# Hybrid block on one core: 128-row score stacks, single scatters per scan step, experts queued behind their last scatter

## The chip, the core and the metric

The kernel runs on one core of a Trainium2 chip. The metric is the device time of one launch in microseconds (us); for more than one run it is their median. TensorE (PE) multiplies matrices into PSUM and has a weight load of its own (PEld). VectorE (DVE), ScalarE (ACT) and GpSimd (POOL) do element-wise work. Each engine runs its instructions in the order of its own queue. Transfers are issued by SyncE (SP), and those with addresses taken from a tensor by GpSimd.

## The reference, cut to what matters

The input is x of 4 sequences x 512 tokens x 128 channels. Each `_layernorm` is over the channels.

```python
x = x + attn_a(layernorm(x), ...)      # state-space scan, then 8 experts, top 2 of each token
x = x + ffn(layernorm(x), ...)         # silu(gate) * up, then down; hidden size 384
x = x + attn_b(layernorm(x), ...)      # causal attention, 16 heads of 8
x = x + ffn(layernorm(x), ...)         # the same weights once more
```

In `attn_a` the scan keeps 256 channels x 16 states for each sequence, `h = dA*h + d*x*B` and `y = sum_n h*C`. Then a router picks two of eight experts for each token, and the output is the weighted sum of the two experts' outputs. In `attn_b` the scores of a head are q (8 numbers) times k (8 numbers), scaled, masked to the past, and put through a softmax.

## The kernel before, in words

**First stage, lines 599 to 1074.** One scan step belongs to one state of one sequence, so there are 4 x 16 = 64 of them, numbered 0 to 63 here. In `scan` (L895) VectorE runs the recurrence over all 2 x 512 positions (`hst`, L910), then the small operations of other work that was begun in this step, then the next step's input (`bx`, L889, which reads a PSUM tile `pb` and an SBUF tile). GpSimd multiplies `hst` by C (`hc`, L922), and TensorE sums the states (`yp`, L867). `hst` has two buffers, so scan step s+2 waits for `hc` of step s. `queued` (L875) makes every other GpSimd instruction traced between two `hc` run between these two. `hc` is also tied to run behind the last small VectorE operation begun in its step (L928).

**The work beside the scan.** Five `Stream` objects (L470) hold generators. In each scan step a stream whose last half-step is done begins its next generator piece, and later in the step ends it. Of the streams that want the PSUM tag "sc", only the first in order moves in a turn (`halves`, L575). The order is `ahead` (`front` of the next sequence: convolution, B and C, step sizes), `closing` (`close`: skip, gate, output projection, router, row numbers; then `start` and `scatter`), `tokens` (`combine`, `first_ffn`, `project`), `tiles` (`experts`, `onward`), and `rest`.

`scatter` (L254) sends each token's row to its two places in a DRAM tensor sorted by expert. That is 8 indirect DMAs for a sequence, issued by GpSimd, two per piece. `experts(g)` (L324) handles a group of sequences (group 0 is sequence 0, group 1 is sequence 1, group 2 is sequences 2 and 3), in 15, 15 and 23 tiles of 128 rows. It begins with `plan` (L270, where each tile begins) and `moved` (L302), then loads rows and the three weight matrices of each tile's expert through SP (L355 to L363), multiplies (L376, L388), and stores rows (L347). `start` (L584) puts it on the tiles stream ahead of `scatter`. `combine` (L395) gathers two rows for each token by 8 indirect DMAs, two per piece, and adds them to `base`. `project` (L502) writes q and k of a sequence, each split into three bf16 parts, to DRAM, and notes them in `stores`.

In `front`, `third` (L778) finishes the bf16 split of B and C in the tile `bc`: a copy of 32 rows (L779) and a subtraction (L780), both by GpSimd.

**Second stage, lines 1077 to 1330.** The heads of a sequence are treated in two units of 8 heads. `fill` (L1120) loads a unit's q and k parts into the stacks `qs` and `ks`, 96 rows high, of which 9 x 8 = 72 hold parts (`NP9`). `maxima` (L1131) multiplies 72 rows (L1145), adds the mask by another matmul (L1149), takes the row maximum with VectorE (L1141), and writes the maxima in three bf16 parts into rows 72 to 74 of `qs` (L1175). The same rows of `ks` hold -1 (L1103). `exps` (L1181) multiplies 75 rows (L1198, L1206) and takes the exponential (L1211). `weigh` (L1214) multiplies by the values (L1225). The streams go on: first whole turns until sequence 0 is in `stores` (L1287), then a turn beside 7 of 10 steps of `exps`, later 5 of 10, and forced turns where a sequence is not in `stores` yet (L1304). `last` is the final feed-forward of a sequence.

PE, VectorE, ScalarE and SP run in program order in the first stage (`ORDERED`, L34). GpSimd, and all engines in the second stage, are ordered by the scheduler.

Of the kernel before, what the change touches and what calls it, by code (L numbers as in the profile page):

```python
# [10 lines left out]
BF16 = mybir.dt.bfloat16  # L11
AF = mybir.ActivationFunctionType
ALU = mybir.AluOpType
# [3 lines left out]
P = 128  # L17
B, L, C = 4, 512, 128
NT = L // P
# [6 lines left out]
NH, HS, KVL = 16, 8, 64  # L26
# [11 lines left out]
def block_kernel(ctx, tc, x, rms1_w, rms2_w, in_proj_w, conv_w, conv_b, x_proj_w,  # L38
# [215 lines left out]
    def scatter(b):  # L254

        g = place[b][0]
        yield
        for t in range(NT):
            for k in range(2):
                done = nc.gpsimd.indirect_dma_start(  # L260
                    sorted_x[g], bass.IndirectOffsetOnAxis(ap=rows[b][:, t, k : k + 1], axis=0),
                    hs[b][:, t, :], None,
                ).ins
                tc.declare_no_dep(done, group=f"rows{g}", reason="no two tokens have the same row")
                tc.add_to_no_dep_group(f"rows{g}", done)
                if k and t < NT - 1:
                    yield
                    yield

# [54 lines left out]
    def experts(g):  # L324


        both, moved = plan(g)
        yield
        yield
        moved()  # L330
        yield
        yield
        n = NTILES[g]
        yield
        yield
        xt, xT, wgu, wd, hidden, ys, of = {}, {}, {}, {}, {}, {}, {}
        for i in range(-1, n + 3):
            if i == 0:
# [56 lines left out]
    def combine(b):  # L395

        g = place[b][0]
        got = []
        for t in range(NT + 2):
            for k, yk in enumerate(got.pop(0) if t > 1 else ()):  # L400
                nc.vector.scalar_tensor_tensor(
                    base[b][:, t - 2, :], yk, gates[b][:, t - 2, k : k + 1],
                    base[b][:, t - 2, :], ALU.mult, ALU.add,
                )
            yield
            new = []
            for k in range(2 if t < NT else 0):
# [5 lines left out]
                new.append(yk)  # L413
            got.append(new)
            yield


# [165 lines left out]

    def start(b):  # L584

        g, i = place[b]
        if i == len(GROUPS[g]) - 1:
            tiles.add(experts(g), onward(g))
        return
        yield  # L590

    def onward(g):
        for b in GROUPS[g]:
# [5 lines left out]
    with ExitStack() as first:  # L599
# [110 lines left out]
        def front(b):  # L710
# [65 lines left out]
                nc.scalar.copy(mid, rest)  # L776

            def third():  # L778
                nc.gpsimd.tensor_copy(bc[b][32:64, :], mid[32:64, :])  # L779
                nc.gpsimd.tensor_tensor(bc[b][64:96, :], rest[64:96, :], mid[64:96, :], ALU.subtract)  # L780

            if b == 0:
# [250 lines left out]
        with tc.manual_schedule(engines=ORDERED):  # L1033
            warm(16)
            moments(xs[0], mv0[:, 0])
            deviations([0])
            for k in range(KW):
                nc.vector.tensor_tensor(w_k[:, k, :], w_in[:, 0:EI], cwb[:, :, k], ALU.mult)
            first = front(0)
            next(first)  # L1040
            next(first)
            moments(xs[1], mv0[:, 1])
            deviations([1])


            w_bc = w1.tile([P, NE, 3, 2 * NS], F32, tag="w_bc", name="w_bc")
            nc.vector.tensor_copy(
                w_bc, w_xp[:, :, DTR:].unsqueeze(2).to_broadcast([P, NE, 3, 2 * NS])
            )
            pick32 = w1.tile([96, 2 * NS], F32, tag="pick32", name="pick32")  # L1050
            nc.vector.tensor_reduce(
                pick32, ident[0:96, 0:96].rearrange("p (g c) -> p c g", g=3), AX.X, ALU.add
            )
            pick = w1.tile([96, 2 * NS], BF16, tag="pick", name="pick")
            nc.vector.tensor_copy(pick, pick32)
            for _ in first:
                pass

            rest, ahead = Stream(early()), Stream()
            streams = [ahead, closing, tokens, tiles, rest]  # L1060
            for b in range(B):
                if b:
                    closing.add(close(b - 1), start(b - 1), scatter(b - 1))
                for n in range(NS):
                    if n == 0 and b + 1 < B:
                        ahead.add(front(b + 1))
                    if n == 8 and b == 0:
                        closing.add(prepared())
                    scan(b * NS + n, streams)
        with tc.manual_schedule(engines=ORDERED):  # L1070
            accumulate(*late.pop(0))
            closing.add(close(B - 1), start(B - 1), scatter(B - 1))
            for _ in range(3):
                turn(closing, tokens, tiles)


    with ExitStack() as second:
# [15 lines left out]

        NP9 = 9 * HS
        NU = NH // 2
        UNITS = 2 * B
        qs, ks = [], []
        for i in range(3):  # L1100
            qs.append(w1.tile([96, NU, L], BF16, tag=f"qs{i}", name=f"qs{i}"))
            k = w1.tile([96, NU, L], BF16, tag=f"ks{i}", name=f"ks{i}")
            nc.sync.dma_start(  # L1103
                k[NP9 : NP9 + 3, :, :], below.unsqueeze(1).to_broadcast([3, NU, L])
            )
            ks.append(k)

        def values(b):
            va, qk = vs[b % 2], stores[b][2]
# [10 lines left out]
        def fill(u):  # L1120

            b, h0 = u // 2, (u % 2) * NU
            q_d, k_d, _ = stores[b]
            for i in range(3):
                at = slice(3 * HS * i, 3 * HS * (i + 1))
                for stack, of in ((qs[u % 3], q_d), (ks[u % 3], k_d[i])):
                    nc.sync.dma_start(
                        stack[at], of[:, :, h0 : h0 + NU, :].rearrange("j d h l -> (j d) h l")
                    )

        def maxima(u):  # L1131
# [4 lines left out]
            for t in range(NT):  # L1136
                w = (t + 1) * P
                n = L // w
                for h0 in range(0, NU, n):
# [3 lines left out]
                    for h in range(h0, h0 + n):  # L1143
                        c = (h - h0) * w
                        nc.tensor.matmul(  # L1145
                            sc[:, c : c + w], q[0:NP9, h, t * P : w], k[0:NP9, h, 0:w],
                            start=(h == h0), stop=False, skip_group_check=True,
                        )
                    nc.tensor.matmul(  # L1149
# [22 lines left out]
            nc.scalar.copy(mT, pm)  # L1172
            m_d = dram.tile([3, NU, L], BF16, tag="m_d", name="m_d")
            nc.gpsimd.dma_start(m_d.rearrange("i h l -> (i h) l"), mT)  # L1174
            nc.gpsimd.dma_start(q[NP9 : NP9 + 3, :, :], m_d)  # L1175
            yield

        scale = float(HS) ** -0.5
# [2 lines left out]
        def exps(G):  # L1181
# [6 lines left out]
            for blocks in (  # L1188
# [198 lines left out]
```

## Time and profile before

| what | value |
|---|---|
| median of 3 runs | 919.38 us (919.25 to 921.01) |
| profiled execution, time | 916.44 us |
| profiled execution, span from first to last instruction | 914.7 us |
| mean granted TensorE clock | 0.872 |
| PE busy | 736.9 us (81%) |
| VectorE busy | 584.6 us (64%) |
| ScalarE busy | 409.4 us (45%) |
| GpSimd busy | 308.1 us (34%) |
| DMA, mean over the span | 108 GB/s |
| scan step 0, 24, 40, 48, 63 begins at | 38.1, 150.6, 232.8, 277.9, 377.1 us |
| first score matmul L1145 | 450.2 us |

Engine rows in the profile count busy time only, without the issuing of transfers. A line of the timeline begins with its start and its length in us; what stands in brackets at its end is how long the engine had been idle before it, and what ended that. In a table of windows, the columns behind the window are busy us of PE, PEld, VectorE, ScalarE and GpSimd with the number of instructions, then the granted TensorE clock (1.00 is full speed), the DMA share and GB/s.

### The profile page before, as it was taken

Reading aid. Unit: us, or ns where it says so; the run is one execution under the profiler, and the core shown is the slowest. Engines: PE = TensorE matmul, PEld = TensorE weight load, DVE = VectorE, ACT = ScalarE, POOL = GpSimd, SP = SyncE. Lnnn points to the kernel's source line nnn. Section 1 sums busy time; section 2 is a strip of 40 time slices with the busy share of each in tenths; the row PEclk is TensorE's granted clock in tenths of the full one; section 3 lists DMA queues with packets and bytes.
Section 4 is the critical chain, followed back from the end, with each engine's and each line's share of the span. In section 5 each row is a group of like instructions: output and inputs, shape, how many; then the busy total and the mean of one; then the engine's idle time right before and its main releaser. Section 6 shows DMA issues by size and latency. Waiting matters only on the chain. (4 is left out here: it accounts for less than half of the span.)

```text
span 914.7 us, 12164 instructions
## 1 busy us (share of the span) xinstructions
PE 736.9 (81%) x3867; PEld 436.0 (48%) x3867; DVE 584.6 (64%) x1160; ACT 409.4 (45%) x793; POOL 308.1 (34%) x242
## 2 busy tenths in 40 slices
PE   8698697699898855976696998898768997799854
PEld 4432242363466512564465576367524454365422
DVE  4799999899998987755364542275534266457311
ACT  3847556556743421342112553413436524546641
POOL 1165755765664467315103013000341402301010
PEclk9898999799999867998668999979968887989977
DMA  5167221361466314426735157627310420600000
GB/s 132 43 220 259 68 58 58 100 204 54 145 183 198 93 57 125 142 80 200 184 130 178 61 173 214 152 68 221 98 29 3 120 64 20 158 2 14 3 13 11
DMA packets 84481, 99.18 MB, mean 108 GB/s; under 512 B 10369, under 2 KB 56457, under 8 KB 83241
## 3 DMA queue, kind: packets, MB, share of 16 engines
q1 hardware_dynamic: 78881, 87.09, 32.4%
q0 software_dynamic: 4352, 10.89, 3.8%
q8 instruction: 31, 0.51, 0.2%
q10 hardware_dynamic: 1184, 0.43, 0.2%
q14 instruction: 33, 0.27, 0.1%
HBM read 76.67 MB, written 21.63 MB: 107 GB/s over the span
## 5 line engine op out<-in xcount | busy, mean ns | idle before, releaser
L922 POOL TENSOR_TENSOR hc<-hst,cs 128x1024 f32<-128x1024 f32 x64 | 150.7, 2355 | 132.1 <-issue 31.6
L867 PE MATMUL yp<-hc,ident 128*128 128x512 f32 x256 | 148.0, 708 | 48.6 <-POOL hc L922 47.4
L910 DVE TENSOR_TENSOR_SCAN hst<-da,bx 128x1024 f32<-128x1024 f32 x64 | 146.4, 2287 | 11.7 <-POOL hc L922 4.6
L1141 DVE TENSOR_REDUCE mx<-sc 128x1 f32<-128x384 f32 (+3 forms) x168 | 102.9, 636 | 59.5 <-PE sc L1149 57.4
L867 PEld LDWEIGHTS yp<-hc,ident 128*128 128x128 f32 x256 | 51.5, 216 | 129.4 <-POOL hc L922 89.3
L1211 ACT ACTIVATE p<-st 128x512 f32<-128x512 f32 x160 | 90.2, 598 | 30.0 <-PE st L1206 26.8
L847 ACT ACTIVATE da<-delta,A 128x512 f32<-128x512 f32 (+1 forms) x128 | 84.8, 714 | 34.3 <-DVE hst L910 26.6
L1145 PE MATMUL sc<-ks,qs 72*128 72x128 bf16 (+3 forms) x256 | 73.5, 347 | 14.8 <-DMA ks<-k_d 7.9
L321 DVE SCALAR_TENSOR_TENSOR thm<-thm,mpg 128x512 f32<-128x512 f32 x53 | 36.1, 681 | 68.1 <-ACT thm L382 68.0
L889 DVE TENSOR_TENSOR bx<-du,pb 128x1024 f32<-128x1024 f32 x64 | 78.2, 1223 | 2.0 <-PE pb L857 0.4
L376 PE MATMUL mpg<-xTm,wgu 128*128 128x128 f32 x424 | 66.9, 300 | 12.2 <-DMA wgu<-in_Wg_dram 7.7
L1198 PE MATMUL st<-qs,ks 75*128 75x512 bf16 (+3 forms) x256 | 63.6, 312 | 11.7 <-ACT p L1211 5.9
L376 PEld LDWEIGHTS mpg<-xTm,wgu 128*128 128x128 f32 x424 | 59.9, 212 | 21.9 <-issue 15.8
L1174 POOL DMA_DIRECT2D m_d<-mT x8 | 4.4, 552 | 183.6 <-ACT mT L1172 183.6
L376 PE MATMUL mpu<-xTm,wgu 128*128 128x128 f32 x424 | 62.7, 294 | 3.0 <-DVE mh L322 3.0
L369 ACT ACTIVATE xTm<-mpt,r2w 128x128 f32<-128x128 f32 x53 | 19.4, 366 | 100.7 <-PE mpt L367 100.7
L388 PE MATMUL mpd<-wd,mh 128*128 128x128 f32 x424 | 60.6, 287 | 1.9 <-ACT xTm L369 0.9
L376 PEld LDWEIGHTS mpu<-xTm,wgu 128*128 128x128 f32 x424 | 57.8, 210 | 5.6 <-DVE mh L322 3.3
L388 PEld LDWEIGHTS mpd<-wd,mh 128*128 128x128 f32 x424 | 54.2, 199 | 5.8 <-ACT xTm L369 3.3
L1149 PE MATMUL sc<-maskq,identb 128*128 128x128 bf16 (+2 forms) x176 | 49.3, 280 | 0.0
L382 ACT ACTIVATE thm<-mpg 128x512 f32<-128x512 f32 x53 | 31.7, 597 | 39.3 <-PE mpg L376 31.6
L321 DVE SCALAR_TENSOR_TENSOR th<-th,pg 128x512 f32<-128x512 f32 x24 | 16.5, 687 | 49.3 <-ACT th L449 49.2
(253 smaller groups left out, 1197.9 us busy)
## 6 DMA issues: line engine op xcount, KB each, us to landing
cs<-c_d SPq DMA_DIRECT2D x64, 256.0 KB
wgu<-in_Wg_dram SPq DMA_DIRECT2D x53, 256.0 KB
wgu<-in_Wu_dram SPq DMA_DIRECT2D x53, 256.0 KB
wd<-in_Wd_dram SPq DMA_DIRECT2D x53, 256.0 KB
xg<-zero SPq DMA_DIRECT2D x8, 1024.0 KB
qs<-q_d SPq DMA_DIRECT2D x24, 192.0 KB
k_d<-parts POOLq DMA_DIRECT2D x12, 384.0 KB
ks<-k_d SPq DMA_DIRECT2D x24, 192.0 KB
```

Source lines behind the costliest of these rows:

```text
L321: nc.vector.scalar_tensor_tensor(th, th, 1.0, g, ALU.add, ALU.mult)
L376: nc.tensor.matmul(pp[:, f, :], w[:, k, f * P : (f + 1) * P], rows_in, start=True, stop=True,)
L388: nc.tensor.matmul(pd, hT[:, f, :], w[:, f, :], start=(f == 0), stop=(f == NFC - 1))
L847: nc.scalar.activation(da[:, e, e:], delta[b][:, e, e:], AF.Exp, scale=A[:, e, n : n + 1])
L867: nc.tensor.matmul(yps[b][:, e, :], ident, hc[:, e, :], start=(n == 0), stop=(n == NS - 1))
L889: nc.vector.tensor_tensor(bxs[s], du[s // NS], taps[s][1].unsqueeze(1).to_broadcast([P, NE, L]), ALU.mult)
L910: nc.vector.tensor_tensor_scan(hst.rearrange("p e l -> p (e l)"), dec.pop(s).rearrange("p e l -> p (e l)"), bxs.pop(s).rearrange("p e l -> ...
L922: done = nc.gpsimd.tensor_tensor(hc, hst, cs.unsqueeze(1).to_broadcast([P, NE, L]), ALU.mult).ins
L1141: nc.vector.tensor_reduce(*taken, AX.X, ALU.max)
L1145: nc.tensor.matmul(sc[:, c : c + w], q[0:NP9, h, t * P : w], k[0:NP9, h, 0:w], start=(h == h0), stop=False, skip_group_check=True,)
L1198: nc.tensor.matmul(pt[:, c : c + L - kt * P], k[0 : NP9 + 3, h0 + j, rows], q[0 : NP9 + 3, h0 + j, kt * P : L], start=(c == 0), stop=False ...
L1211: ready[G] = nc.scalar.activation(p, pt, AF.Exp, scale=scale).ins
```

## The change

Four edits are made together.

1. `qs` and `ks` are 128 rows high. VectorE clears rows 64 to 127 of each of the six tiles when a stack is first filled. The maxima and the -1 rows are now rows 125 to 127. `maxima` multiplies 125 rows and `exps` all 128, with zeros in rows 72 to 124.
2. `scatter` moves on after every single scatter (for the last sequence after every two, as before), and `combine` of sequence 0 gathers one row per piece instead of two.
3. `experts` no longer plans. `plan` and `moved` go to the tiles stream ahead of the scatters, and `experts` and `onward` are put there behind the group's last scatter.
4. The copy of 32 rows of `bc` is done by ScalarE instead of GpSimd.

```diff
@@ scatter
-                if k and t < NT - 1:
+                if (k or b < B - 1) and (k, t) != (1, NT - 1):
                     yield
                     yield
@@ new, beside experts
+    def planned(g):
+        plans[g], moved = plan(g)
+        yield
+        yield
+        moved()
+        yield
@@ experts
-        both, moved = plan(g)
-        yield
-        yield
-        moved()
-        yield
-        yield
+        both = plans.pop(g)
         n = NTILES[g]
-        yield
-        yield
@@ combine
-        for t in range(NT + 2):
-            for k, yk in enumerate(got.pop(0) if t > 1 else ()):
+        n = 2 if b else 1
+        which = [(t, k) for t in range(NT) for k in range(2)]
+        for i in range(0, len(which) + 2 * n, n):
+            for yk, t, k in got[max(i - 2 * n, 0) : max(i - n, 0)]:
@@ start
-        if i == len(GROUPS[g]) - 1:
-            tiles.add(experts(g), onward(g))
-        return
-        yield
+        full = i == len(GROUPS[g]) - 1
+        if full:
+            tiles.add(planned(g))
+        yield from scatter(b)
+        if full:
+            tiles.add(experts(g), onward(g))
@@ third, in front
-                nc.gpsimd.tensor_copy(bc[b][32:64, :], mid[32:64, :])
+                nc.scalar.copy(bc[b][32:64, :], mid[32:64, :])
@@ scan loop, twice
-                    closing.add(close(b - 1), start(b - 1), scatter(b - 1))
+                    closing.add(close(b - 1), start(b - 1))
@@ stacks
-        NP9 = 9 * HS
+        NP9, MXR = 9 * HS, P - 3
-            qs.append(w1.tile([96, NU, L], BF16, tag=f"qs{i}", name=f"qs{i}"))
-            k = w1.tile([96, NU, L], BF16, tag=f"ks{i}", name=f"ks{i}")
-            nc.sync.dma_start(
-                k[NP9 : NP9 + 3, :, :], below.unsqueeze(1).to_broadcast([3, NU, L])
-            )
-            ks.append(k)
+            qs.append(w1.tile([P, NU, L], BF16, tag=f"qs{i}", name=f"qs{i}"))
+            ks.append(w1.tile([P, NU, L], BF16, tag=f"ks{i}", name=f"ks{i}"))
@@ fill
+            if u < 3:
+                for stack in (qs[u], ks[u]):
+                    nc.vector.memset(stack[KVL:P], 0.0)
+                nc.sync.dma_start(ks[u][MXR:P], below.unsqueeze(1).to_broadcast([3, NU, L]))
@@ maxima
-                            sc[:, c : c + w], q[0:NP9, h, t * P : w], k[0:NP9, h, 0:w],
+                            sc[:, c : c + w], q[0:MXR, h, t * P : w], k[0:MXR, h, 0:w],
-            nc.gpsimd.dma_start(q[NP9 : NP9 + 3, :, :], m_d)
+            nc.gpsimd.dma_start(q[MXR:P, :, :], m_d)
@@ exps
-                        pt[:, c : c + L - kt * P], k[0 : NP9 + 3, h0 + j, rows],
-                        q[0 : NP9 + 3, h0 + j, kt * P : L],
+                        pt[:, c : c + L - kt * P], k[:, h0 + j, rows],
+                        q[:, h0 + j, kt * P : L],
```

More of the change, by code (lines that the diff above doesn't have):

```diff
@@ L322, in halved @@
         nc.vector.scalar_tensor_tensor(dst, th, 0.5, other, ALU.mult, ALU.mult)
-    def experts(g):
-        both, moved = plan(g)
+    plans = {}
+    def planned(g):
+        plans[g], moved = plan(g)
         yield
@@ L331, in experts @@
         yield
-        yield
+    def experts(g):
+        both = plans.pop(g)
         n = NTILES[g]
-        yield
-        yield
         xt, xT, wgu, wd, hidden, ys, of = {}, {}, {}, {}, {}, {}, {}
@@ L397, in combine @@
         g = place[b][0]
+        n = 2 if b else 1
+        which = [(t, k) for t in range(NT) for k in range(2)]
         got = []
-        for t in range(NT + 2):
-            for k, yk in enumerate(got.pop(0) if t > 1 else ()):
+        for i in range(0, len(which) + 2 * n, n):
+            for yk, t, k in got[max(i - 2 * n, 0) : max(i - n, 0)]:
                 nc.vector.scalar_tensor_tensor(
-                    base[b][:, t - 2, :], yk, gates[b][:, t - 2, k : k + 1],
-                    base[b][:, t - 2, :], ALU.mult, ALU.add,
+                    base[b][:, t, :], yk, gates[b][:, t, k : k + 1], base[b][:, t, :],
+                    ALU.mult, ALU.add,
                 )
             yield
-            new = []
-            for k in range(2 if t < NT else 0):
+            for t, k in which[i : i + n]:
                 yk = wt.tile([P, C], F32, tag="yk", name="yk", bufs=6)
@@ L412, in combine @@
                 )
-                new.append(yk)
-            got.append(new)
+                got.append((yk, t, k))
             yield
@@ L1071, in block_kernel @@
             accumulate(*late.pop(0))
-            closing.add(close(B - 1), start(B - 1), scatter(B - 1))
+            closing.add(close(B - 1), start(B - 1))
             for _ in range(3):
```

## The prediction

> **What bounds the kernel now.** I read the table of windows first: from 40 to 320 us VectorE is busy 34 to 38 of every 40 us (32.4 and 26.4 in the two windows behind, where the scan ends), then TensorE takes over with 26 to 38 of 40. So the scan stage is read from the queues of VectorE and GpSimd, the second stage from TensorE and its clock.
>
> GpSimd's timeline where sequence 0 is scattered:
>
> ```profile
> 159.46 2.36 POOL L922 TENSOR_TENSOR hc<-hst,cs 128x1024 f32<-128x1024 f32 x1
> 161.99 1.01 POOL L260 DMA_INDIRECT xg<-hs,rows  x1 [0.17 <-issue]
> 163.30 0.96 POOL L260 DMA_INDIRECT xg<-hs,rows  x1 [0.30 <-issue]
> 165.90 0.97 POOL L779 COPY bc<-bc_mid 32x512 bf16<-32x512 bf16 x1 [1.64 <-DMA xg<-hs,rows]
> 166.93 1.15 POOL L780 TENSOR_TENSOR bc<-bc_rest,bc_mid 32x512 bf16<-32x512 f32 x1
> 168.16 2.35 POOL L922 TENSOR_TENSOR hc<-hst,cs 128x1024 f32<-128x1024 f32 x1
> ```
>
> VectorE's, of the same place:
>
> ```profile
> 163.00 2.29 DVE L910 TENSOR_TENSOR_SCAN hst<-da,bx 128x1024 f32<-128x1024 f32 x1
> ...
> 170.54 2.29 DVE L910 TENSOR_TENSOR_SCAN hst<-da,bx 128x1024 f32<-128x1024 f32 x1 [3.00 <-POOL hc L922]
> 172.75 3.68 DVE L833 TENSOR_TENSOR du<-du,sp_d 128x1024 f32<-128x1024 f32 x1
> ...
> 179.90 1.20 DVE L836 TENSOR_TENSOR delta<-delta,du 128x1024 f32<-128x1024 f32 x1
> ```
>
> A bare scan step lasts 3.75 us on VectorE (2.29 + 1.22 and gaps). Two scatters and a product are 4.82 us on GpSimd (154.64 to 159.46), and the bc pair waits until scatters have landed. The scan at 170.54 so waits 3.00 us, and `du` takes 3.68 where `delta`, of the same shape, takes 1.20: GpSimd's product ran from 172.99 to 175.34. For sequence 2, gathers join: products start at 335.93, 343.37, 350.81, 358.24, each 7.44 apart.
>
> The second stage, in the table of windows (busy PE, PEld, DVE, ACT, POOL; clock; DMA; GB/s):
>
> ```profile
> 446.00:450.00 4.00, 0.00 (x0) 0.00 (x0) 0.00 (x0) 0.00 (x0) 0.00 (x0) 0.50 0.80 189
> 450.00:454.00 4.00, 3.72 (x19) 2.20 (x20) 2.37 (x4) 0.00 (x0) 0.00 (x0) 0.50 0.86 178
> 458.00:462.00 4.00, 3.54 (x13) 1.52 (x12) 3.49 (x7) 0.00 (x0) 0.00 (x0) 0.50 0.91 292
> 462.00:466.00 4.00, 3.75 (x12) 1.40 (x11) 3.81 (x6) 0.00 (x0) 0.00 (x0) 0.50 0.00 0
> 466.00:470.00 4.00, 3.95 (x21) 3.34 (x20) 2.08 (x7) 0.37 (x1) 0.00 (x0) 0.50 0.02 4
> 474.00:478.00 4.00, 4.00 (x35) 3.65 (x35) 2.06 (x3) 1.37 (x5) 0.00 (x0) 1.00 0.63 193
> 875.00:880.00 5.00, 4.05 (x25) 1.19 (x26) 0.00 (x0) 1.41 (x3) 0.00 (x0) 0.52 0.00 0
> ```
>
> From 450 to 466 TensorE is 90% busy with 72-row score matmuls and stays at half clock. At 466.9 expert tiles with 128 rows begin, and within 5 us the clock is full.
>
> **The change part by part: single scatters.** One scatter and a product are 2.35 + 0.17 + 1.0 = 3.52 us, under 3.75, so GpSimd keeps up. For steps 24 to 33 I laid both queues out with the row durations. Before they run from 150.56 to 203.10. After, step 24 is as before; L780 waits for the scatter ahead of it (1.64 us after its issue here, 2.32 at 248.90), so `hc` of step 26 starts near 164.6, the queue behind it (next product, TensorE's sum, scan two steps on) is late, and one VectorE operation is still held, about 1.8 us; then nothing more. Step 34 begins at 194.9 instead of 203.1, or -8.2. Of it 4.6 is only work put off: four tiles' pairs L321/L322, 1.15 us each (4.90 - 3.75). Steps 40 to 47 took 45.1; their VectorE floor, with five tiles instead of six and the same 1.8, is 41.4: -3.7.
>
> Steps 48 to 62 took 99.2. After, summed from the same rows: step 48 6.0, 49 4.9, 50 9.0 (stall kept), 51 7.2, 52 4.9, 53 5.95 + 1.15, 54 4.4 + 1.15, 55 5.55 + 1.15, 56 and 57 4.9 each, 58 3.75, 59 with the plan 6.7, 60 4.5, 61 and 62 with scatter and gather 4.8 each: 85.8, or -13.4. The 7.44 us steps go; they did not need gathers so soon.
>
> **bc by ScalarE.** GpSimd loses 0.60 to 0.97 us three times in the scan; step 11 (`sp_d` held until 90.08) gains 0.7, the others lie inside the sums. ScalarE gains 0.5 to 0.6 each (nearest row: bc_mid, 0.61), hidden by its idle time (9.2 us before 179.23); without that cover 2 us. In the prologue one takes the other's place: 0, between -0.6 and +0.6.
>
> Scan step 63 so begins at 377.1 - 8.2 - 3.7 - 13.4 - 0.7 = 351, with 15 expert tiles done instead of 17 and `combine` of sequence 0 barely begun.
>
> **Experts later.** What was put off comes before attention. The built order has 14 tiles between scan and first maxima (before: 8), and 15 turns after the first three until sequence 0 is stored (before: 6). A turn with a tile costs 4.2 us by the nearest stretch: six tiles from 399.4 to 424.6, with close(3) and project(0) inside. SP's six transfers and two value loads of a tile (up to 5.3 us with a cs) move along with it, and three feed-forward turns without a tile cost 3.5 each. Sum: 15 x 4.2 + 10 + 3 (rest of the 7.2 us stall at 431.85, since scatters no longer sit between project's GpSimd steps) + 8 (stack loads, 442 to 450) + 5 (clears, below) = 89, against 73.1 before. The bounds are 3.8 a turn (tiles alone, 604 to 650: 12 in 46 us) and 6.6 (all turns from 377 to 437: 9 in 60). I take 4.2, since close(3) and project were inside it. First maxima: 351 + 89 = 440 instead of 450.2, with 29 tiles done instead of 25.
>
> To the fifth exponential group (656.3) it took 206.1 with 28 tiles; four fewer at 3.8 are -15.
>
> **128 rows.** The rows do not set a matmul's length: at full clock L1149 with 128 rows takes 0.38 for 512 columns, and so does L1198 with 75. In the maxima VectorE is busy 3.4 to 3.8 of 4 us, so there a faster TensorE gains little. The gain is behind them: tile work at half clock from 466.9 to 471.8 (2.2), L1225 at 585.1 (3.99 against 2.36: 1.6), tiles from 604 to 609.6 (2.2), 702 to 713 (11 us at half, I count 3), 760 to 766 (2.5, I count 1), L1225 at 876.9 (4.49 against 2.36: 2.1). That is 12, in three stretches of 6, 3 and 3. The Trainium skill (TensorE: Matmul & The Clock Gate, Part 1) says the full clock comes after about 3.4 us of sustained matmuls[...]. By that rule the gain is 0. The row above denies it: 16 us at 0.50 with 72 rows, full within 5 us with 128. But the added rows are zeros, and no row shows what zeros do to the clock. Bounds 0 to 16; I take 12, by the row. A loss is excluded as long as no wait is added.
>
> **Clears.** Six of 64 x 2048 elements: the nearest VectorE row is L889, 1.22 for 1024, so up to 2.4 each; GpSimd's clear of 1024 took 0.95. VectorE is busy 26.4 of 40 and 23.4 of 40 us there. Queued behind each are the tiles' L321 and L322, then L388; I put 5 on the path, bounds 0 to 15. The -1 rows' transfer on SP now waits for a clear, and weight loads are queued behind it: 0 to 6, inside the 5. Against it speaks a rule of the skill (SBUF — State Buffer, SBUF: two separate sides): a VectorE operation in a 2-port mode shuts GpSimd out for its whole length, also from writing descriptors. The row of `du` shows the lock the other way round. By the rule six clears delay GpSimd's scatters by up to 15, by GpSimd's rows (17.8 of 40 busy, 400 to 440) most falls in idle time. I add nothing.
>
> **Sum.** Span: 440 + 206.1 - 15.2 - 6 = 625 (before 656.3); to the ninth group 114.5 - 3 = 111.5; the rest 143.9 - 3 = 141. Together 877.5 against 914.7. The profiled execution adds 1.74 (916.44 - 914.7), and the median of the runs lies 2.94 above it: 882.
>
> **The rivals.** (A) The sum, 882, its own range 870 to 892, chance 0.50. (B) Zeros don't count for the clock, so the tall stacks do not do what they are there for: 894, chance 0.20; for it the rule, against it nothing but the row of real data. (C) The overlap is better: the five forced turns ahead of the seventh group are gone in the built order, and TensorE's idle 670.5 to 678.3 (yk gathers, then a norm) and the waits around it shrink: 15 less, 867, chance 0.17. (D) The turns before attention stay at 6.6 us, as they were with their chains through ScalarE and VectorE, and the clears come on top (15 / 18 = 0.8): 18 x 7.4 + 8 = 141 us instead of 89, so +52, 934; slower. It decides from 89 + 37 = 126 us, or 6.6 a turn with the clears' share in it ((126 - 8) / 18). Against it: the stretch at 4.2. Chance 0.08. (E) In between, 919: 0.05.
>
> **Numbers.** 882. Within 0.2% is about what this kernel's measurement can tell from no change. Range 862 to 904: A, B and C, leaving out D, E and the tails. Faster 0.88, same 0.03, slower 0.09.
>
> **What would show it.** `hc` of steps 25 to 32 about 3.8 us apart, `du` at 1.2; step 63 at 348 to 355; first L1145 at 430 to 450 with 29 tiles; granted clock above 0.5 in the maxima-only stretch and at the last L1225. Step 63 above 365 breaks the scan part; a first L1145 above 465 is D; clock 0.50 through the maxima is B.

## The result, and the profile after

The changed kernel takes 906.48 us, the median of 4 runs (901.97 to 908.82), beside 920.19 us for the kernel before on the same chip. The ratio is 0.9865, with a 95% interval of 0.9824 to 0.9906. It is faster by 1.35%, little more than a third of what was forecast (882 us, and 904 at the end of the range). The profiled execution took 908.82 us with a span of 907.1, the slowest of the four; in its trace the forecast span of 877.5 is missed by 29.6 us. Mean granted clock 0.895 (before 0.872), PE busy 715.0 us (before 736.9). The ratios here use executions in the chip's faster state alone, and the one profiled execution in its slower state, that of e3 below (919.67 us against a median of 910.85), is not used for the last stretch.

I read the trace of the changed kernel, called "after", stage by stage; `...` marks lines left out. First the scan, GpSimd's timeline where sequence 0 is scattered:

```profile
157.47 2.35 POOL L928 TENSOR_TENSOR hc<-hst,cs 128x1024 f32<-128x1024 f32 x1 [0.62 <-DVE bc_rest L781]
159.98 1.00 POOL L260 DMA_INDIRECT xg<-hs,rows  x1 [0.15 <-ACT bc_mid L782]
163.25 1.15 POOL L786 TENSOR_TENSOR bc<-bc_rest,bc_mid 32x512 bf16<-32x512 f32 x1 [2.27 <-DMA xg<-hs,rows]
164.48 3.40 POOL L928 TENSOR_TENSOR hc<-hst,cs 128x1024 f32<-128x1024 f32 x1
168.02 0.99 POOL L260 DMA_INDIRECT xg<-hs,rows  x1
169.03 2.37 POOL L928 TENSOR_TENSOR hc<-hst,cs 128x1024 f32<-128x1024 f32 x1
```

And VectorE's of the same place:

```profile
162.26 2.29 DVE L916 TENSOR_TENSOR_SCAN hst<-da,bx 128x1024 f32<-128x1024 f32 x1
...
167.91 2.29 DVE L916 TENSOR_TENSOR_SCAN hst<-da,bx 128x1024 f32<-128x1024 f32 x1 [1.10 <-POOL hc L928]
170.11 2.38 DVE L839 TENSOR_TENSOR du<-du,sp_d 128x1024 f32<-128x1024 f32 x1
```

The pair of scatters ahead of each product is gone, and the scan waits 1.10 us for `hc` where it waited 3.00. One wait of GpSimd is left, ahead of L786 (2.27 us), and `du` still takes 2.38 us beside a product. Scan step 63 begins at 356.51 (before 377.11).

Then the clears. This is VectorE in the norm of close(3), the last link before the router of sequence 3:

```profile
382.21 0.17 DVE L974 TENSOR_SCALAR rms_v<-ss 128x4 f32<-128x4 f32 x1 [1.51 <-ACT hs L967]
...
384.07 1.76 DVE L1128 MEMSET ks<- 64x2048 uint32 x1 [0.48 <-issue]
385.87 0.16 DVE L143 TENSOR_TENSOR rs_t<-rs_r 128x4 f32<-128x4 f32 x1
...
388.04 1.76 DVE L1128 MEMSET qs<- 64x2048 uint32 x1 [0.47 <-issue]
...
397.05 1.76 DVE L1128 MEMSET ks<- 64x2048 uint32 x1 [0.48 <-issue]
398.85 0.24 DVE L145 SCALAR_TENSOR_TENSOR rs_r<-rs_t,rs_r 128x4 f32<-128x4 f32 x2
```

TensorE's timeline behind it:

```profile
399.56 1.35 PE L176 MATMUL pt<-ident,hs 128*128 128x128 f32 x4 [10.83 <-ACT hs L977]
...
478.56 0.59 PE L1151 MATMUL sc<-ks,qs 125*128 125x128 bf16 x4 [5.52 <-DMA ks<-k_d]
```

The same chain in VectorE's timeline of before:

```profile
395.71 0.16 DVE L968 TENSOR_SCALAR rms_v<-ss 128x4 f32<-128x4 f32 x1
...
397.89 0.16 DVE L145 SCALAR_TENSOR_TENSOR rs_r<-rs_t,rs_r 128x4 f32<-128x4 f32 x1
```

Five of the six clears stand between `rms_v` and `rs_r`. Each costs 1.76 us and 0.48 us before it, and tile work slips in as well. The chain from `rms_v` takes 16.6 us from start to start, where it took 2.18 before. TensorE, in order, sits idle 10.83 us in front of the transpose that needs it. The first score matmul comes at 478.56, not at 440.

Last the clock, in the table of windows of after (columns as before: busy PE, PEld, VectorE, ScalarE, GpSimd; clock; DMA; GB/s):

```profile
482.00:486.00 4.00, 2.82 (x17) 1.48 (x16) 3.94 (x8) 0.00 (x0) 0.00 (x0) 1.00 0.95 216
486.00:490.00 4.00, 2.88 (x14) 1.35 (x14) 3.99 (x9) 0.00 (x0) 2.21 (x3) 1.00 0.84 262
...
615.00:620.00 5.00, 3.69 (x18) 1.73 (x18) 4.99 (x10) 0.00 (x0) 0.00 (x0) 1.00 0.00 0
```

In these stretches with maxima alone, where the clock was 0.50 before, it is now 1.00. TensorE is done early in them (2.8 of 4 us) and VectorE is the full engine (3.94 of 4).

### The profile page after: what moved, and what is told of

It reads as the page before. It is cut to its first block, busy times and chain, and to the rows that moved or that the text cites. A ratio compares the mean times of both kernels' runs of the same rounds, so it can differ in the third digit from the quotient of the medians.

```text
span 907.1 us, 12174 instructions
## 1 busy us (share of the span) xinstructions
PE 715.0 (79%) x3857; PEld 431.2 (48%) x3867; DVE 578.8 (64%) x1166; ACT 411.3 (45%) x797; POOL 307.7 (34%) x238
## 5 line engine op out<-in xcount | busy, mean ns | idle before, releaser
L873 PE MATMUL yp<-hc,ident 128*128 128x512 f32 x256 | 145.2, 695 | 47.7 <-POOL hc L928 45.5
L873 PEld LDWEIGHTS yp<-hc,ident 128*128 128x128 f32 x256 | 51.5, 215 | 128.4 <-POOL hc L928 87.2
L1217 ACT ACTIVATE p<-st 128x512 f32<-128x512 f32 x160 | 89.8, 599 | 38.6 <-PE st L1212 36.6
L1151 PE MATMUL sc<-ks,qs 125*128 125x128 bf16 (+3 forms) x256 | 66.1, 313 | 28.3 <-DVE mx L1147 19.3
L321 DVE SCALAR_TENSOR_TENSOR thm<-thm,mpg 128x512 f32<-128x512 f32 x53 | 36.2, 683 | 75.8 <-ACT thm L384 75.7
L378 PEld LDWEIGHTS mpg<-xTm,wgu 128*128 128x128 f32 x424 | 58.9, 208 | 18.7 <-issue 8.4
L1204 PE MATMUL st<-qs,ks 128*128 128x128 bf16 (+3 forms) x246 | 58.9, 306 | 9.3 <-ACT p L1217 5.1
L413 POOL DMA_INDIRECT yk<-yg,rows_y x32 | 31.0, 970 | 91.6 <-DMA yg<-ym 61.9
L260 POOL DMA_INDIRECT xg<-hs,rows x32 | 33.6, 1049 | 45.9 <-DVE cmove L305 39.9
L321 DVE SCALAR_TENSOR_TENSOR th<-th,pg 128x512 f32<-128x512 f32 x24 | 16.5, 687 | 49.0 <-ACT th L452 49.0
```

Of the source, the lines that this page charges most:

```text
L378: nc.tensor.matmul(pp[:, f, :], w[:, k, f * P : (f + 1) * P], rows_in, start=True, stop=True,)
L873: nc.tensor.matmul(yps[b][:, e, :], ident, hc[:, e, :], start=(n == 0), stop=(n == NS - 1))
L1151: nc.tensor.matmul(sc[:, c : c + w], q[0:MXR, h, t * P : w], k[0:MXR, h, 0:w], start=(h == h0), stop=False, skip_group_check=True,)
L1204: nc.tensor.matmul(pt[:, c : c + L - kt * P], k[:, h0 + j, rows], q[:, h0 + j, kt * P : L], start=(c == 0), stop=False, skip_group_check=True,
L1217: ready[G] = nc.scalar.activation(p, pt, AF.Exp, scale=scale).ins
```

## The experiments

Each ratio is to the kernel before on the same chip; a difference of 1% is about 9.2 us. From each trace I took four moments: the start of scan step 63, the first expert tile whose `mh` is made after it, the first score matmul, and the end. They split what follows the scan into three stretches:

| kernel | step 63 | to first tile | tile to first score | first score to end | ratio to before (95%) |
|---|---|---|---|---|---|
| before | 377.1 | (overlap) | 73.1 in all | 464.5 | 1 |
| after | 356.5 | 18.2 | 103.8 | 428.5 | 0.9865 (0.9824 to 0.9906) |
| e1 clears by GpSimd | 354.7 | 18.2 | 93.3 | 426.9 | 0.9747 (0.9683 to 0.9811) |
| e2 stacks alone | 377.4 | (overlap) | 89.4 in all | 450.6 | 0.9995 (0.9972 to 1.0018) |
| e3 no stacks | 355.2 | 18.2 | 87.2 | not used | 0.9905 (0.9881 to 0.9929) |
| e4 clears, 72 rows | 356.5 | 18.2 | 101.1 | 445.3 | 1.0035 (0.9996 to 1.0074) |
| e5 experts behind, alone | 375.5 | (overlap) | 87.3 in all | 470.1 | 1.0135 (1.0022 to 1.0248) |
| e6 gathers in pairs | 355.9 | 21.4 | 95.8 | 443.9 | 1.0028 (1.0005 to 1.0051) |
| e7 clears twice | 355.9 | 18.2 | 116.5 | 431.1 | 1.0060 (1.0033 to 1.0088) |
| e8 clears late | 354.7 | 18.3 | 105.5 | 423.2 | 0.9879 (0.9830 to 0.9927) |
| e9 last product first | 356.7 | 18.7 | 104.5 | 422.1 | 0.9851 (0.9810 to 0.9892) |
| e11 zeros by DMA, 53 rows | 357.4 | 18.5 | 125.8 | 473.2 | 1.0690 (1.0631 to 1.0750) |
| e12 GpSimd, in pieces | 356.4 | 18.2 | 91.6 | 429.3 | 0.9775 (0.9679 to 0.9871) |
| e13 the same, late | 355.7 | 18.2 | 94.9 | 430.9 | 0.9806 (0.9723 to 0.9890) |
| e14 DMA, 48 rows | 355.7 | 18.6 | 87.9 | 423.9 | 0.9628 (0.9572 to 0.9685) |
| e15 DMA, 32 rows | 354.0 | 18.6 | 87.7 | 426.2 | 0.9707 (0.9676 to 0.9738) |
| e16 DMA, 16 rows | 356.9 | 18.7 | 86.1 | 438.3 | 0.9786 (0.9754 to 0.9818) |
| e17 DMA, 48 and 5 rows | 354.0 | 18.6 | 94.6 | 430.4 | 0.9889 (0.9820 to 0.9958) |

**The edits taken apart.** Four kernels: clears moved to GpSimd; the stacks alone on the kernel before; the change without the stacks; the change with its clears but with 72 and 75 rows multiplied.

e1:

```diff
-                    nc.vector.memset(stack[KVL:P], 0.0)
+                    nc.gpsimd.memset(stack[KVL:P], 0.0)
```

> The changed kernel with its six clears issued on GpSimd instead of VectorE, nothing else. Theory T1 (the clears cost what they hold up: the norm behind close(3) took 16.6 us on VectorE with clears of 1.76 us between its links, 2.06 before, and TensorE idled 10.83 us behind it): that chain is short again, the idle 10.83 us before pt<-hs goes, the first score matmul comes 10 to 14 us before 478.6, the time falls to 892 to 897. Rival T2 (the order of turns sets the first score matmul, and the clears only fill time in which VectorE would have waited): first scores within 3 us of 478.6, time 903 to 910. Rival T3 (GpSimd is slow at clears and its scatters of sequence 3 wait behind them, above 20 us): 915 or more.

0.9747 (893.37 us), first scores at 466.2: T1. But GpSimd's clears are not free either. VectorE's timeline of e1:

```profile
380.72 3.45 DVE L136 TENSOR_SCALAR rs_t<-rms_v 128x4 int32<-128x4 int32 x1
...
384.20 3.46 DVE L139 TENSOR_SCALAR rs_r<-rs_t 128x4 int32<-128x4 int32 x2
...
388.04 0.68 DVE L321 SCALAR_TENSOR_TENSOR thm<-thm,mpg 128x512 f32<-128x512 f32 x1
```

GpSimd's:

```profile
380.60 3.54 POOL L1128 MEMSET ks<- 64x4096 bf16 x1
384.09 3.54 POOL L1128 MEMSET qs<- 64x4096 bf16 x1
```

Two integer links that take 0.17 us alone took 3.45, and each ends when a clear on GpSimd ends (384.1, 387.6). `thm`, at 0.68 us beside the next clear, was not held. This is the lock between VectorE and GpSimd of which the Trainium skill (SBUF — State Buffer, SBUF: two separate sides) says that whoever starts first keeps it for the whole instruction. The prediction asked what VectorE's clears do to GpSimd; here GpSimd's clears hold VectorE, the direction that its row of `du` had shown.

e2, the kernel before with edit 1 alone:

> The kernel before with the 128-row stacks and the clears by VectorE alone; scatters, gathers, bc and the start of the experts as before. T1: the clock gain of about 12 us and a cost of clears of 5 to 15 us before the first scores nearly cancel, 913 to 923, with the granted clock at 1.0 in the stretch with maxima alone (0.50 before, 450 to 466). T2 (clears free, clock gain whole): 905 to 909. If the rise of the clock is worth little because VectorE bounds the maxima: 921 to 932.

0.9995 (916.91 us): the two nearly cancel, as T1 had it. The first scores come 16.3 us later after step 63 than before (89.4 against 73.1), and the rest is 13.9 us shorter (450.6 against 464.5).

e3, the change without edit 1 (the stack lines of the diff undone):

> The changed kernel without the 128-row stacks and without the clears: 72 and 75 rows again, the other three edits kept. T1: loses the clock gain of 12 us and the cost of clears of about 12, so within 5 us of the changed kernel, 902 to 912, its first scores at 464 to 469 and the clock at 0.50 through its maxima. T2 (clears free): 916 to 921, first scores at 476 to 481.

0.9905 (910.85 us), within 0.4% of the changed kernel, as T1 had it: edit 1 as a whole brings next to nothing, since its gain is paid back by its clears. The first scores came at 460.7, some 3 us sooner than expected.

e4, the clears kept, the rows not used:

```diff
-        NP9, MXR = 9 * HS, P - 3
+        NP9, MXR = 9 * HS, 9 * HS
...
-                        pt[:, c : c + L - kt * P], k[:, h0 + j, rows],
+                        pt[:, c : c + L - kt * P], k[0 : NP9 + 3, h0 + j, rows],
...
```

The second operand is cut to 75 rows in the same way, and the -1 rows and the maxima go to rows 72 to 74.

> The changed kernel with tall, cleared stacks, but the -1 rows and the maxima back in rows 72 to 74 and the matmuls over 72 and 75 rows. Clears and order as in the changed kernel, so the difference to it is the granted clock alone. By the sum of the prediction 12 us slower than the changed kernel: 916 to 921, clock 0.50 in the maxima. Rival: TensorE's busy time fell by 21.9 us between the kernels, all of it counts: 926 to 930. Rival: VectorE or ScalarE bound these stretches: 904 to 909.

1.0035. The 922.91 us lie in none of the three ranges, nearest to the first (916 to 921). Against e3 the clears cost 1.3%, or 12 us; against the changed kernel the clock is worth 1.7%, or 15.6 us (16.8 in the traces behind the first score). The table of windows of e4, at the place of 615 to 620 above:

```profile
619.00:624.00 5.00, 4.47 (x17) 2.00 (x16) 4.27 (x9) 0.00 (x0) 0.00 (x0) 0.50 0.00 0
```

The same work, with 72 rows instead of 125: half clock.

**Experts behind the last scatter, alone** (e5, the kernel before with edit 3):

> The kernel before with one edit alone: the experts of a group begin behind its last scatter. Scatters and gathers stay in pairs, bc stays on GpSimd, the stacks stay at 96 rows. Theory T4 (the single scatters and gathers carry the gain in the scan): step 63 of the scan stays at 374 to 378, the first scores come about 104 us later (as without stacks and clears), near 480, and the whole takes 922 to 932. Rival (what the scan gains is only expert work put off, which this edit alone would put off too): step 63 near 357 to 366 and 908 to 914.

1.0135, slower. Step 63 stays at 375.5, as T4 had it, but this does not show what T4 concludes. At step 63 the trace of e5 has 17 tiles done, as many as before (15 in the changed kernel), so this edit alone put no tile off. By the prediction's 1.15 us for a tile's pair L321/L322, the two tiles put off in the changed kernel are 2.3 of the 20.6 us that its scan gained, an estimate; what the gathers and feed-forward pieces put off are worth was not measured. The opposite combination, single scatters without edit 3, was not run. My first scores at 480 were wrong: they came at 462.8.

**Gathers in pairs again** (e6, `n = 2` in `combine` for every sequence):

> The changed kernel with sequence 0's gathers in pairs again (all other edits kept). Combine of sequence 0 then takes four turns fewer, so attention begins about four turns earlier. If the first scores are late because of the turns before them (each 4.6 us with a tile in it, 84 us of the 104 without clears), they come at 458 to 464 instead of 478.6. Theory T1 on the total (the tiles put off are done later in the same time, TensorE is busy on both sides): time within 5 us of the changed kernel, 901 to 911. Rival (turns ahead of attention are lost time): 886 to 893. Rival (hc of step 63 is held longer by more gathers, nothing else): 908 to 913.

1.0028 (920.86 us), outside all three ranges, and the first scores came at 473.2, not at 458 to 464. The built order has four turns fewer before attention (11 instead of 15), and three turns forced in ahead of the seventh exponential group, for which sequence 2's projection isn't ready. The first scores come 5.4 us earlier, the rest takes 15.4 us longer. From the first score to the end, after and then e6 in the table of windows:

```profile
478.56:907.10 428.54, 344.50 (x2353) 214.75 (x2363) 211.86 (x561) 182.53 (x363) 72.84 (x81) 0.90 0.31 86
473.16:917.10 443.94, 359.10 (x2444) 226.81 (x2455) 217.24 (x568) 187.55 (x375) 72.85 (x81) 0.92 0.32 90
```

TensorE is busy 14.6 us longer in e6 and idle just as long (84.8 and 84.0 us). So it is the work put off that makes the rest longer (27 tiles are done before the first score, against 30), not waits around the forced turns. Single gathers are worth some 1.6%, though nearly nothing of that is saved in the scan (step 63 at 355.9). Why four turns fewer saved only 5.4 us before the first score stays open.

**Are the clears late enough, or dear anywhere?** e8 makes them wait for the last scatter; e7 does each twice.

```diff
...
-                    nc.vector.memset(stack[KVL:P], 0.0)
+                    ins = nc.vector.memset(stack[KVL:P], 0.0).ins
+                    tc.add_manual_dep(ins, last_scatter[0].name, behind, reason="clears late")
```

> The changed kernel with the six clears on VectorE made to wait for the last scatter of sequence 3, so that none can fall among the links of close(3)'s norm. T1: the norm is 2 to 4 us again, TensorE's idle 10.83 us is gone, first scores at 462 to 468, and since neither engine's clear blocks the norm, a bit better than clears on GpSimd, where integer links of the norm still took 3.45 us instead of 0.17: 886 to 893. Rival: the clears now hold up VectorE's tile work and the stack loads by as much: 899 or more.

0.9879 (905.79 us): no gain over the changed kernel, the rival's range. The norm was short again and the scatters began at 401.81 instead of 418.73, but the clears then fell into the feed-forward part. VectorE's timeline of e8:

```profile
416.41 1.76 DVE L1131 MEMSET ks<- 64x2048 uint32 x1 [0.48 <-DVE th L324]
418.21 0.69 DVE L325 SCALAR_TENSOR_TENSOR fh<-th,pu 128x512 f32<-128x512 f32 x1
```

TensorE's:

```profile
415.98 2.07 PE L451 MATMUL pg<-xT,fwg 128*128 128x512 f32 x2 [6.58 <-DVE th L324]
```

TensorE waits 6.58 us for `th`, which stands behind the first clear, and more behind the next ones. T1 in the form "only the norm's links cost" fell here: VectorE's queue is in order, and at both places something on TensorE's path stands behind the clears.

> The changed kernel with each of the six VectorE clears done twice. T1 (VectorE's clears lie on the path wherever they fall, since putting them behind the scatters changed nothing): 12 to 16 us more, 918 to 923, first scores at 490 to 496. Rival (only their place among the norm's links costs, and the second clear of each pair adds 1.8 us to it once or twice): 908 to 912.

1.0060, or 18 us above the changed kernel by the ratios (14.6 in the traces), with the first scores at 490.6: T1. A second set of six clears (13.4 us of VectorE's time with the gaps) costs 12.7 us in the stretch before the scores. In this stage a clear on VectorE costs nearly its whole length on the path.

**Clears on GpSimd in pieces** (e12: eight of 64x512 for each; e13: the same, behind the last scatter):

> Clears on GpSimd, each in eight pieces of 64x512. With whole clears two links of the norm (integer operations on VectorE, 0.17 us) took 3.45 us each, until a clear of GpSimd ended. Theory (a VectorE operation of that kind waits for the GpSimd instruction that runs, so it waits for a piece of about 0.5 us instead of 3.5): the chain of close(3) falls by 5 to 6 us, first scores at 460 to 462, 887 to 890. Rival (it waits for the whole row of clears, or the pieces cost more in all than they free): 893 to 900.

The mechanism held. VectorE's timeline of e12:

```profile
382.10 0.53 DVE L974 TENSOR_SCALAR rms_v<-ss 128x4 f32<-128x4 f32 x1 [1.28 <-ACT hs L967]
...
382.66 0.46 DVE L136 TENSOR_SCALAR rs_t<-rms_v 128x4 int32<-128x4 int32 x1
...
383.15 0.47 DVE L139 TENSOR_SCALAR rs_r<-rs_t 128x4 int32<-128x4 int32 x2
```

0.46 instead of 3.45, since a piece ends every 0.47 us. The operation held need not be an integer one: `rms_v`, a `TENSOR_SCALAR` in f32 (0.17 in the changed kernel), takes 0.53. The time did not follow: 0.9775, in the rival's range, and 91.6 us to the first scores against 93.3. Of the 6 us that the two links gained, 1.7 are left at the end of the stretch; where the others went was not traced.

> As the one before, with the pieces placed behind the last scatter of sequence 3 in GpSimd's queue, when GpSimd is idle but for one addition until project(0). Theory: no link of close(3) meets a clear, 885 to 889. Rival: 48 pieces of 0.5 us behind the scatters delay GpSimd's addition x<-base,fo and the projection of sequence 0, which is on the path: 895 or more.

0.9806 (899.50 us), in the rival's range; not told apart from e1.

**The last product** (e9: the scatter and gathers ahead of step 63's product put behind it):

> The changed kernel with the scatter and the three gathers that stand ahead of the last step's product put behind it. The product is at 360 instead of 364.56, and TensorE's last sum of the scan begins at about 363 instead of 366.95. If that chain (product, sum, y, out projection, norm) sets the first scores: they come 4 us earlier, 902.5 for the whole. Rival: the tiles' chain in the same turns sets it, no change: 906.5.

0.9851, no change (904.70 us). GpSimd's timeline of e9:

```profile
361.98 2.33 POOL L932 TENSOR_TENSOR hc<-hst,cs 128x1024 f32<-128x1024 f32 x1 [2.20 <-DVE base L406]
...
372.07 0.94 POOL L413 DMA_INDIRECT yk<-yg,rows_y  x1 [0.30 <-issue]
373.04 2.34 POOL L955 TENSOR_TENSOR y<-y,sz 128x1024 f32<-128x1024 f32 x1
```

The product is at 361.98 (364.56 in the changed kernel), but the gathers then stand ahead of `y`, which begins at 373.04 (372.26). GpSimd's queue has that work to do in any order.

**Zeros by DMA.** No engine clears; rows 72 onward are written from a small tile of zeros on SP's queue. e11 writes 53 rows a stack:

```diff
...
-                    nc.vector.memset(stack[KVL:P], 0.0)
+                    nc.sync.dma_start(
+                        stack[NP9:MXR], nought.unsqueeze(1).to_broadcast([MXR - NP9, NU, L])
+                    )
```

> The changed kernel with the rows 72 to 124 of the stacks zeroed by six DMAs from a small tile of zeros on SP's queue, no clear on VectorE or GpSimd. T1: no engine is held, the norm is 2 to 4 us, first scores at 461 to 467, 886 to 893. Rival: 2.6 MB more through the DMA engines (they are 13 to 85% busy there) and six more issues on SP ahead of the weights delay the tiles: 897 to 903.

1.0690 (978.68 us), far worse than either. SP's queue in e11:

```profile
412.04 14.94 SPq L1130 DMA_DIRECT2D ks<-nought  x1
427.03 18.07 SPq L1133 DMA_DIRECT2D ks<-below  x1
```

The table of windows there:

```profile
435.00:445.00 10.00, 0.00 (x0) 0.00 (x0) 0.00 (x0) 0.00 (x0) 0.00 (x0) 0.50 0.07 24
```

The DMA engines are 7% busy, about one of sixteen, and move 24 GB/s; 424 KB at that rate are 18 us, and the weights behind wait (TensorE idle for 27.15 us). The Trainium skill (DMA: Bandwidth & Descriptors, Why a DMA increments its semaphore by 16 and not by 1) says that a copy runs on the largest number of engines up to 16 that divides the size of the outermost dimension on both sides. For 53 rows that is 1, which agrees with the 7%. e14, e15 and e16 take 48, 32 and 16 rows:

> The changed kernel with zeros by DMA, 48 rows of them instead of 53 (120 rows in the maxima, 123 in the exponentials). If 53 rows went through one of the 16 DMA engines because 53 does not divide among them (7% busy, 24 GB/s), 48 rows go at 150 GB/s or more, 2.6 us each, TensorE's wait of 27 us is gone, no engine clears, and first scores come 87 to 91 us behind the first tile after the scan, as without clears: 885 to 892, the clock as with 125 rows. Rival (rows of 1 KB from a broadcast source are slow whatever their number): 960 or more.

0.9628: 886.84 us, as the first case had it, the best version found and faster than both kernels. The rival is out. SP passes the two transfers in 1.4 us:

```profile
411.16 0.75 SPq L1130 DMA_DIRECT2D qs<-nought  x1
411.97 0.65 SPq L1130 DMA_DIRECT2D ks<-nought  x1
```

The stretch to the first scores is 87.9 us, as without clears (87.2 in e3). So the zeroing costs next to nothing by itself; the in-order engine that did it cost 16 us. The clock did not do all that was expected of it, as the table below shows.

> As the one before with 32 rows of zeros: 104 rows in the maxima, 107 in the exponentials. If the clock needs only somewhat more than 75 rows: as with 48, within 4 us. If the clock asks for nearly all rows: the maxima stay at 0.50 and the time is 12 to 17 us above that of 48 rows.

0.9707. By the medians 3.0 us above e14 and in the trace 2.3 behind the first score, the first case; by the ratios 7 us, between the two cases. The clock of its first maxima was mostly 0.50.

> As the one before with 16 rows of zeros: 88 rows in the maxima, 91 in the exponentials. If the number of rows counts by degrees, the maxima lie between 0.50 and 1.00 here; if there is a step, they show one of the two. Time 900 to 906 with the clock at 0.50, 885 to 892 at 1.00.

0.9786 (897.09 us, some 3 under the range for a clock of 0.50): 14.4 us behind e14 after the first score. The first maxima show 0.50, as with 72 rows, yet 88 rows are worth something: the stretch behind the first score is 7.0 us shorter than with 72 rows in e4 (438.3 against 445.3), and the ratio is 1.2% below that of e3.

e17 has 125 and 128 rows again, with transfers of 48 and 5 rows:

> The changed kernel with its full 128 rows and zeros by DMA in two transfers a stack, 48 rows and 5. The clock in the maxima as in the changed kernel (1.00), where 120 rows showed 0.50 to 0.88; the way from the first tile after the scan to the first scores as with 48 rows alone (88 us). If the two add up: 877 to 886. Rival (the five rows go through few DMA engines and hold up the queue like the 53 did): 890 to 910.

0.9889 (901.89 us): the two don't add up, and the time lies in the rival's range. The rival's cause does not show: before the first score SP's queue passes each of the transfers of zeros in at most 1.72 us. The first scores come 94.6 us behind the first tile, and the clock in its maxima was not full, as the next table shows. Why it loses 6.7 us ahead of the first score against e14, and 6.5 behind it, stays open.

**The clock against the rows.** The granted clock behind the first score, read from the tables of windows:

| rows in the maxima | kernels | granted clock in the first 20 us or so | mean to the end |
|---|---|---|---|
| 72 | before, e4, e5 | 0.50 for 19 us or more | 0.82 to 0.85 |
| 88 | e16 | 0.50 for 24 us | 0.85 |
| 104 | e15 | 1.00 from 4 to 7.5 us, back at 0.50 | 0.88 |
| 120 | e14 | 1.00 from 6 to 9 us, back at 0.50 | 0.89 |
| 125 | after, e2, e6, e8, e9, e12, e13 | 1.00 after 3 to 6 us, for 20 us or more | 0.90 to 0.92 |
| 125 | e1, e11, e17 | 1.00 after 4 to 6 us, back at 0.50 within 20 | 0.88 to 0.90 |
| 125 | e7 | 0.50 for 20 us | 0.88 |

The whole way from the first score to the end with 72 (e4), 88 (e16), 104 (e15) and 120 rows (e14), beside the line of after above with 125:

```profile
475.81:921.10 445.29, 368.50 (x2363) 225.02 (x2363) 213.68 (x561) 182.66 (x363) 72.75 (x81) 0.83 0.30 83
461.63:899.90 438.27, 361.87 (x2373) 223.24 (x2373) 214.53 (x562) 184.99 (x366) 72.76 (x81) 0.85 0.32 86
460.17:886.40 426.23, 350.97 (x2373) 218.40 (x2373) 213.89 (x562) 184.76 (x366) 72.69 (x81) 0.88 0.33 90
462.09:886.00 423.91, 346.87 (x2373) 215.28 (x2373) 214.23 (x562) 184.72 (x366) 72.80 (x81) 0.89 0.34 91
```

For nearly the same instructions TensorE's busy time falls from 368.5 to 344.5 us as the rows go from 72 to 125. More rows, zeros among them, lift the clock, by degrees over the whole stage; in the first maxima the full height makes 1.00 likely, not certain. What throws it back in the last two rows of the table I can't tell from these runs.

## Why the prediction was wrong

**The scan** gained 20.6 us of the 26 summed. Steps 24 to 33 took 47.9 us (forecast 44.3), steps 40 to 47 took 43.4 (41.4), steps 48 to 62 took 85.7 (85.8), and step 24 began 0.72 sooner (bc, 0.7). Step 63 is 5.5 us late, from the first two. What the layout left out is that TensorE's sums wait as well: step 32 took 7.97 us (6.02 before), with waits of 1.65 for `pb` and 1.49 for `yp`.

**"Sum: 15 x 4.2 + 10 + 3 (...) + 8 (...) + 5 (clears, below) = 89"** is the step that failed; it was 122.1. Two terms of it:

- The tail of the scan is missing. In every kernel with the other edits and single gathers, 18.2 to 18.7 us pass between step 63 and the first tile: GpSimd's last product, TensorE's sum at half clock, `y`. In the kernel before, a tile and feed-forward pieces were done in that time, and my stretch of 4.2 us a turn began behind it, at 399.4. So I priced the turns and left out the time in which they hardly advance. GpSimd's gathers lengthen it: `hc` of step 63 comes 8.05 us after its scan, 4.58 before, and e9 shows that behind the product they hold up `y` instead.

After, VectorE's, GpSimd's and TensorE's lines of that time:

```profile
356.51 2.29 DVE L916 TENSOR_TENSOR_SCAN hst<-da,bx 128x1024 f32<-128x1024 f32 x1 [0.48 <-DVE bx L895]
364.56 2.34 POOL L928 TENSOR_TENSOR hc<-hst,cs 128x1024 f32<-128x1024 f32 x1
366.95 3.78 PE L873 MATMUL yp<-hc,ident 128*128 128x512 f32 x4 [3.33 <-POOL hc L928]
374.72 0.67 DVE L322 SCALAR_TENSOR_TENSOR mh<-thm,mpu 128x512 f32<-128x512 f32 x1
```

Before, the last sum, and the tile with which the stretch of 4.2 us a turn begins:

```profile
384.93 1.88 PE L867 MATMUL yp<-hc,ident 128*128 128x512 f32 x4
399.36 0.33 PE L367 MATMUL mpt<-ident,xt 128*128 128x128 f32 x1 [1.02 <-ACT fo L459]
```

- The clears are mis-sized: 5 in the sum, 15.9 measured (103.8 in the changed kernel, 87.9 with zeros by DMA), and 16.3 in e2. The mechanism, "queued behind each are the tiles' L321 and L322", was named. I then let the wait fall into idle time because VectorE was busy 26 of 40 us. It is an in-order queue; in e7 12.7 of 13.4 us of clears come out at the other end. My upper bound of 15 was about the value. The lock by which VectorE's clears would delay GpSimd's scatters was not put to the test: the last clear ends at 398.8, the first of these scatters begins at 418.73, and no row showed that a clear runs in a 2-port mode.

The turns themselves were right: without engine clears, tile to first score takes 87.9 us where the sum without clears has 84. Together 5.5 + 18.2 + 10.9 + 3.9 = 38.5, which is, but for rounding, the first score's delay of 38.6 (478.6 against 440).

**128 rows**: the row was the better guide than the rule. The Trainium skill's page on the clock gate (TensorE: Matmul & The Clock Gate, Part 1) speaks of sustained matmuls and time and does not name rows, so I had 0 by it; e4 shows TensorE busy 4.47 of 5 us at 0.50 with 72 rows, and the runs gave 15.6 us by the ratios of e4 and after, where 12 were summed. Rival B is out. Its doubt wasn't idle, though: with 125 rows the clock is not always granted.

**Behind the first score** I had 437.5 us and it took 428.5: to the fifth exponential group 181 (forecast 185), on to the ninth 103 (111.5), and the rest 144 (141). The middle, with the forced turns that rival C named, took 114.5 before and 108.6 in e4, which has the changed order but 72 rows: so 6 us of the gain there go with the order and 5.5 with the rows, where 3 were summed. Rival C's 15 us of shorter waits did not come: TensorE is idle 22.1 us of the middle before, 17.7 in e4 and 20.9 after, and e6, with three turns forced in again, took 100.6.

**Rival D**, slower by 52 us if turns stay at 6.6 us, decided from 126 us. The 122.1 measured is close under it, but not by its mechanism: the turns were short, and the tail and clears made up the rest. The sum in the span: -9.0 behind the first score and +38.6 ahead of it are the 29.6 us missed.

**What the change is worth by part**, from the ratios: experts behind the last scatter alone +1.35%, single scatters and gathers and bc on top of it -2.3% (to e3), the clears +1.3% (to e4), the clock -1.7% (to after). With 48 rows of zeros by DMA the last two together become -2.8% (e14 against e3).

## What to carry to other kernels

Work put on an in-order engine is hidden only if nothing on the path stands behind it in that queue; here a busy share of 26 in 40 us hid almost nothing, so price it at its full length and look for a queue that has no such follower. When work is moved ahead of a stage, sum the stage from its first event, the tail of the one before included, not from a stretch in the middle of it. Work put off ahead of a stage comes back behind it: e6 saved 5.4 us before the first score and paid 15.4 after it.

## What the runs showed of the hardware

- A transfer of 53 rows ran at 24 GB/s with 7% of the DMA engines busy and held SP's queue for 33 us; 48 rows of the same shape left the queue in 0.65 to 0.75 us.
- A clear of 64x4096 bf16 took 1.76 us on VectorE (as 64x2048 uint32), plus 0.48 idle before it, and 3.5 us on GpSimd. While GpSimd cleared, a `TENSOR_SCALAR` of VectorE waited for the end of the running clear (int32, 0.17 became 3.45 in e1 and 0.46 with pieces in e12; f32, 0.53 in e12); a `SCALAR_TENSOR_TENSOR` of 128x512 f32 with one input in PSUM kept its 0.68.
- Rows of zeros count for the granted clock: in the first maxima 72 and 88 rows stayed at 0.50 for about 20 us with TensorE some 90% busy, 104 and 120 reached 1.00 for about 3.4 us, and 125 held it for 20 us or more in seven of eleven kernels. Over the whole way behind the first score the mean was 0.82 to 0.85 with 72 rows and 0.88 to 0.92 with 125.
